# Cross-attention and quantized FFN on one core: row transposes by 32x32 blocks and DRAM instead of DMA transposes, the last projection by rows, and a new order of all steps

## The chip, the core and the metric

The kernel runs on one core of a Trainium2 chip. The metric is device time in microseconds, from several runs of one launch. The engines are named as in the profile: PE multiplies matrices (PEld are its weight loads), DVE and ACT are the vector and the scalar engine, POOL is the general one, and SP issues nearly all DMAs. Each engine works through its own list in order. A difference of about 0.2% is what a measurement of this kernel can tell from none.

## What is computed

Eight batches of 112 rows of 512 go through one layer of cross-attention (16 heads of 128, 375 context rows of 256) and a feed-forward part that works on rounded numbers:

```python
q = rmsnorm(layernorm(x) @ Wq);  k = rmsnorm(ctx @ Wk);  v = ctx @ Wv     # per head
x = x + softmax(q k^T / sqrt(128)) v @ Wo
# feed-forward, n = layernorm(x)
n_q = round(n * 127 / rowmax|n|)                 # per row
h   = gelu((n_q @ W1_q.T) * scales + B1)
h_q = round(h * 127 / rowmax|h|)                 # per row
x   = x + (h_q @ W2_q.T) * scales + B2
```

W1 and W2 are rounded with one maximum for each whole matrix.

## The kernel before, in words

**Tiling.** Batches go in four pairs (NPAIR, BP = 2). For each pair the 16 heads go in four groups of four (NG, HG), so there are 16 groups G, and a unit u is one group of one batch (32 of them). The feed-forward part has 2048 hidden columns in four pieces of 512. A batch has 112 rows in a tile of 128; the 16 spare rows of batches 1 to 7 carry the 112 rows of batch 0.

**Steps of a unit.** Keys (`keys`, L650), copy, squares, sums, root, norm; then keys are turned: DVE transposes 32x32 blocks (L698), four DMAs write them to DRAM (`ks`, L707) and one reads them back in order (`kf`, L714). Queries (L532) take the same way through DRAM (`qt`, `qs`, `qf`). Scores (L758), exponentials on ACT (L780), scaling (L791), blocks on DVE (L797), DRAM (`ps`, `pf`), weighing of the context (`weigh`, L860), values (L887) and projection (`project`, L910), which sums into aT, the transposed output, on DVE (`project_add`, L926). After a pair's last group its aT goes back to rows the same way (`rz`, `rs`, `rf`, `rn`).

**The last pair.** It uses PE transposes in place of the way through DRAM where there is nothing left to hide it: probabilities of the last unit (`pt`, `pk`), and for each batch i of the last pair: values `O{i}`, their copy `U{i}`, projection `P{i}`, its add into aT `A{i}`, transposes of aT `ra` (L965), the residual add `rb` (L1001).

**Feed-forward of a batch b.** `st` takes row means and variances, `fa` to `fd` the root (ln and exp on ACT, the rest on DVE), `fi` (norm_in, L1032) the normed rows and their maximum, `fq` rounds them to bf16. The rounded rows of batches 1 to 5 are transposed by a DMA transpose (`td`, L1073), those of 6 and 7 by PE (`ti`, `tj`). (`b` counts 1 to 7: the rows of batch 0 ride along.) Hidden pieces `h0` to `h3` (L1080), their scale and bias on DVE `i0` to `i3` (L1089), Gelu on ACT (`ge`, or `g0` to `g3` by pieces for the last pair), maximum (`lm`; `mx`, `es`), rounding (`qh0`, `qh1`; `qp`, `qq`), transpose (`te`, the second DMA transpose, L1073; by PE `tp`, `tk` for the last pair), output product (`y0`, `y1`; `Y0` to `Y3`, L1159), `yo` and `yd` the sum and the store.

**What sets the order.** Four strings of words at the end (L1214 to L1364), one for each pair, list all steps in one order, `name.index`; a negative index belongs to the pair before. `play` calls them, and `in_written_order` ties each instruction of PE, DVE, ACT and SP behind the one before it on its engine. So nothing overtakes, and SP's DMAs go out in the list's order. Tiles with the same tag share buffers, so a step can also wait until an earlier user of its tag has been read.

Of the kernel before, what the change touches and what calls it, by code (L numbers as in the profile page):

```python
# [9 lines left out]
F32 = mybir.dt.float32  # L10
# [20 lines left out]
def xattn_ffn_kernel(  # L31
# [16 lines left out]
    nc = tc.nc  # L48
# [853 lines left out]
    def project(G, lo, n, c0):  # L902
        if n == TP:
            after(("u0", G), ("u1", G))
        else:
            after((f"U{lo // S}", G))
        pw = T["pw", G, lo, c0] = mm_tile(f"pw_{G}_{c0}_{lo}")
        for c in range(c0, c0 + NW // n):
            for h in range(HG):
                nc.tensor.matmul(  # L910
                    pw[:, (c - c0) * n : (c - c0 + 1) * n], T["wo", G][:, h, c * P : (c + 1) * P],
                    T["oT", G][:, h, lo : lo + n], start=(h == 0), stop=(h == HG - 1),
                )
# [13 lines left out]

    for n in range(2):
        step(f"o{n}", NG, values, 0, TP, 2 * n)
        step(f"u{n}", NG, value_keep, 0, TP, 2 * n)  # L930
        step(f"p{n}", NG, project, 0, TP, 2 * n)
        step(f"a{n}", NG, project_add, 0, TP, 2 * n)
        step(f"O{n}", NG, values, n * S, S, 0)
        step(f"U{n}", NG, value_keep, n * S, S, 0)
        step(f"P{n}", NG, project, n * S, S, 0)
        step(f"A{n}", NG, project_add, n * S, S, 0)
# [19 lines left out]
    def turn_sum(b):  # L956

        p, i = divmod(b, BP)
        if p == NPAIR - 1:
            after((f"A{i}", NGG - 1))  # L960
        else:
            after(("a0", p * NG + NG - 1), ("a1", p * NG + NG - 1))
# [50 lines left out]
    def stats(b):  # L1013
        after(("rb" if b >= B - BP else "rn", b), ("zf", b))
# [4 lines left out]
    def row_absmax(src, name):  # L1019
        m = small.tile([P, 1], F32, tag="rowmax", name=name)  # L1020
# [8 lines left out]
    def norm_in(b):  # L1029
        after(("fd", b))  # L1030
        xn = T["xn2", b] = ffn.tile([P, C], F32, tag="y", name=f"xn2_{b}")
        nc.vector.tensor_scalar(xn, x2_of(b), T["mv2", b][:, 0:1], T["rstd2", b], ALU.subtract, ALU.mult)  # L1032
        T["m1", b] = row_absmax(xn, f"m1_{b}")
        T["d1", b] = dequant_scale(T["m1", b], absw1, f"d1_{b}")
# [6 lines left out]
    def quantize_in(b):  # L1041
        quantize_rows(home("xq", b, [P, C], BF16), T["xn2", b], quant_scale(T["m1", b], P))
# [27 lines left out]
    def send_rows(b, what):  # L1070

        to = home(what + "T", b, [P, KC if what == "xq" else KF, P], BF16)
        nc.sync.dma_start_transpose(out=to, in_=T[what, b])  # L1073

    def hidden(b, n):
# [3 lines left out]
        for k in range(KC):  # L1079
            nc.tensor.matmul(  # L1080
                ph, T["xqT", b][:, k, :], w1q[:, k, bass.ts(n, NW)], start=(k == 0), stop=(k == KC - 1)
            )

    def hidden_keep(b, n):
        after(("lb", 0))
# [27 lines left out]
    def pieces_scale(b):  # L1113
        after(*[(f"mx{n}", b) for n in range(NF4)])
        m = small.tile([P, 1], F32, tag="rowmax", name=f"m2_{b}")
# [31 lines left out]
    def output(b, k0, n):  # L1147
# [10 lines left out]
        for k in range(k0, k0 + n):  # L1158
            nc.tensor.matmul(  # L1159
                T["py", b], T["hqT", b][:, k, :], w2q[:, k, :], start=(k == 0), stop=(k == KF - 1)  # L1160
# [26 lines left out]
    step("fi", BP, norm_in)  # L1187
    step("fq", BP, quantize_in)
# [3 lines left out]
    step("td", BP, send_rows, "xq")  # L1192
    step("te", BP, send_rows, "hq")
# [13 lines left out]
    for n in range(2):  # L1207
# [7 lines left out]
        cz.0 lk.0 cz.1 lf.0 lf.1 lx.0 l7.0 gl.0 lc.1 kh.0 jl.0 lk.1 lq.0 jl.3 jl.6 kh.1 xs.1 xs.0 xa.1  # L1215
        xc.1 xs.7 ct0.0 kc0.0 xa.0 xb.7 k0.1 kc1.0 xb.1 xd.1 xc.0 xm.1 xa.7 kq0.0 xc.7 k1.1 kr0.0 kq1.0
        kc2.0 xb.0 xd.0 kc0.1 kr1.0 ck0.0 ct0.1 xm.0 kq2.0 xt.1 xd.7 kc1.1 cz.2 xt.0 kr2.0 ck0.1 k2.1
        kb.0 ka.0 xm.7 ke.0 kq0.1 kd.0 xk.0 kn2.0 xt.7 xk.1 gm.0 kn0.0 kv2.0 xk.7 jm.0 kc2.1 xl.0 kv0.0
        kq1.1 lq.1 k0.2 kw0.0 kw2.0 kn1.0 xy.0 xy.1 kr0.1 kv1.0 kr1.1 kq2.1 Q0.0 kr2.1 kb.1 ka.1 jm.3
        kc0.2 ke.1 Q1.0 qt0.0 kw1.0 qs0.0 lx.1 kd.1 jl.1 kn1.1 qv0.0 kn0.1 S0.0 kt0.1 k1.2 kq0.2 kn2.1  # L1220
        S1.0 kt2.1 qw0.0 sa.0 sb.0 kc1.2 kt1.1 k2.2 kq1.2 ks.1 qt1.0 sc.0 qx0.0 sd.0 qv1.0 kr0.2 kc2.2
        k0.3 kr1.2 kq2.2 qs1.0 kr2.2 lc.2 s2.0 lv.0 kb.2 s7.0 ct1.0 qw1.0 lk.2 s1.0 qx1.0 ck1.0 s3.0
        jm.1 kc0.3 s0.0 ka.2 kq0.3 k1.3 ke.2 x0.0 kf.1 k2.3 kc1.3 ly.0 x1.0 e0.0 jl.7 Q0.1 kd.2 e2.0
        kn2.2 e3.0 kn0.2 e1.0 iv.0 xs.3 n0.0 kc2.3 kn1.2 pt0.0 n2.0 k0.4 qt0.1 S0.1 xs.2 qs0.1 n3.0
        kt0.2 kq1.3 pt2.0 pt3.0 pk0.0 kt1.2 n1.0 s1.1 kt2.2 pk2.0 ct1.1 cb0.2 kc0.4 ks.2 s0.1 cb1.2
        pt1.0 kr0.3 s3.1 kr1.3 kq0.4 k1.4 xa.3 pk3.0 jl.2 ck1.1 kr0.4 kq2.3 pk1.0 k2.4 x0.1 xb.3 s2.1
        e0.1 kr2.3 Q1.1 kc1.4 kb.3 ka.3 kc2.4 ke.3 kq1.4 kd.3 kq2.4 kn0.3 xc.3 kf.2 e1.1 x1.1 qf0.1 k0.5
        lq.2 kt0.3 lk.3 e2.1 kn2.3 e3.1 w0.0 xd.3 iv.1 kr1.4 n0.1 n2.1 z0.1 xa.2 qt1.1 w1.0 n1.1 n3.1
        kn1.3 qs1.1 S1.1 z1.1 z3.1 k1.5 z2.1 sb.1 G0.1 xm.3 ps.1 v0.0 kt1.3 s1.2 kr2.4 s2.2 kb.4 ka.4
        kt2.3 ke.4 s0.2 sa.1 xc.2 ks.3 sc.1 s3.2 kc0.5 sd.1 kc1.5 x0.2 k2.5 kq0.5 x1.2 e0.2 lo.0 Q0.2  # L1230
        kq1.5 kr0.5 kc2.5 e3.2 kd.4 kn0.4 kq2.5 e2.2 kn1.4 v1.0 qt0.2 S0.2 k0.6 pf.1 qf1.1 e1.2 cs.2
        Q1.2 kt0.4 qs0.2 kn2.4 kt2.4 iv.2 k1.6 kt1.4 n1.2 kf.3 n0.2 kr1.5 ks.4 n3.2 xb.2 z0.2 S1.2 xd.2
        jm.2 kc0.6 n2.2 lq.3 w0.1 xm.2 G1.1 sa.2 kc1.6 k2.6 qt1.2 qf0.2 z3.2 w1.1 ja.0 z1.2 sb.2 z2.2
        kr2.5 s1.3 v1.1 cz.3 lc.3 v0.1 s2.3 ps.2 ka.5 o0.0 sc.2 js.0 s0.3 kb.5 u0.0 js.1 qs1.2 ke.5 k0.7
        kc2.6 kq1.6 kd.5 s3.3 kn0.5 s7.1 o1.0 x0.3 lk.4 kf.4 kt0.5 e0.3 Q0.3 x1.3 kq0.6 e1.3 kn2.5 u1.0
        G0.2 kr0.6 e2.3 kn1.5 k1.7 kt2.5 pf.2 kt1.5 kr1.6 kc0.7 ks.5 e3.3 k2.7 iv.3 cb0.3 n1.3 qt0.3
        n2.3 Q1.3 lv.1 kc1.7 cb1.3 qs0.3 sd.2 kc2.7 js.2 n0.3 kq2.6 kq0.7 kr2.6 n3.3 qf1.2 s3.4 kr0.7
        ka.6 S0.3 s1.4 z0.3 s0.4 ke.6 z3.3 kq1.7 z1.3 p0.0 kq2.7 z2.3 S1.3 x0.4 ps.3 jr.0 s2.4 sa.3 jr.1
        lk.5 p1.0 kf.5 qt1.3 x1.4 G1.2 qs1.3 w0.2 e0.4 kr2.7 e1.4 kb.6 kd.6 kr1.7 qf0.3 k0.8 pf.3 a0.0
        ka.7 e3.4 lo.1 a1.0 e2.4 sb.3 az.0 k1.8 iv.4 kb.7 n0.4 kn2.6 v0.2 kn0.6 sc.3 kt0.6 z0.4 s3.5  # L1240
        s2.5 xu.2 s1.5 kn1.6 G0.3 s0.5 n3.4 kt2.6 qf1.3 w1.2 n2.4 xv.2 z3.4 kt1.6 z2.4 kc0.8 x0.5 ke.7
        w0.3 ks.6 n1.4 kc1.8 sd.3 kq0.8 jr.2 v1.2 w1.3 e0.5 cs.3 z1.4 G1.3 k2.8 v1.3 v0.3 xu.3 xw.2 jl.4
        x1.5 o0.1 ps.4 kd.7 e2.5 kn0.7 o1.1 kc2.8 kn2.7 kq1.8 kf.6 kn1.7 lq.4 k0.9 js.3 xv.3 xk.2 k1.9
        u0.1 kr0.8 u1.1 xy.2 kr1.8 e3.5 cf.2 kt0.7 s7.2 e1.5 k2.9 kq2.8 iv.5 kt1.7 n2.5 kt2.7 p1.1 n3.5
        cz.4 kr2.8 kc0.9 kq0.9 jm.4 kc1.9 n0.5 pf.4 kc2.9 n1.5 z0.5 ka.8 kq1.9 z3.5 z2.5 kb.8 z1.5 s1.6
        kr0.9 ps.5 s0.6 jr.3 kq2.9 s3.6 p0.1 x0.6 kr2.9 e0.6 kr1.9 ke.8 e1.6 xw.3 jm.6 s2.6 lx.2 Q0.4
        s7.3 ks.7 kd.8 kb.9 a1.1 a0.1 w0.4 qt0.4 S0.4 kn0.8 kn2.8 x1.6 k0.10 pf.5 kn1.8 e2.6 k1.10 xk.3
        ka.9 xy.3 v0.4 xs.4 jl.5 w1.4 qs0.4 xb.4 xa.4 k2.10 kt0.8 lv.2 kt1.8 kf.7 lk.6 kt2.8 kc0.10 ks.8
        xc.4 w0.5 e3.6 xd.4 ke.9 iv.6 kc1.10 kd.9 xs.5 lo.2 w1.5 v0.5 jm.7 kc2.10 v1.4 kq0.10 co0.2 Q1.4
        qf0.4 xa.5 n3.6 n0.6 n2.6 z0.6 v1.5 z3.6 n1.6 jm.5 kq1.10 o1.2 S1.4 s0.7 z1.6 kn0.9 s1.7 kn2.9  # L1250
# [151 lines left out]
```

## Time and profile before

| what | us |
|---|---|
| median of 3 runs (720.21 to 721.2) | 720.77 |
| the profiled run | 720.28 |
| its span, first to last instruction | 718.5 |
| PE busy / DVE busy / ACT busy in it | 702.7 / 537.3 / 433.6 |
| DMA queues, share of 16 engines | 85.1% |
| granted PE clock | 0.999 |

A matmul's end in the profile is modelled, and matmuls overlap: one of 512 columns in f32 is drawn 593 ns long, while the next one starts 429 ns after it. The pace is the distance of the starts, which the chain of work (the profile's fourth part, and its long form in order of time) gives: there each piece counts only up to the start of the next. The idle time of PE is what is left of a stretch after its busy time.

DMA issues that bear on the change (KB of one, median us from issue to landing):

```
rd<-rz SPq DMA_DIRECT2D x24, 64.0 KB, 4.5
rt<-rd SPq DMA_DIRECT2D x6, 256.0 KB, 4.3
xqT<-xq SPq DMA_TRANSPOSE x5, 2.9
hqT<-hq SPq DMA_TRANSPOSE x5, 5.6
```

### The profile page before, as it was taken

The page shows a single profiled execution, that of the slowest core. Times are in us where ns is not written, and L with a number is a line of the kernel's source. Part 1 is how long each engine was busy: PE and PEld are TensorE (multiplying, and loading weights), DVE is VectorE, ACT ScalarE, POOL GpSimd, SP SyncE. Part 2 cuts the span into 40 slices and gives each one's busy share as a digit, 9 for nine tenths or more (in the row PEclk, how much of TensorE's full clock was granted, in tenths as well). Part 3 has the DMA queues.
Part 4 walks back from the last instruction along what each step waited for, and adds up shares of the span by engine and source line. Part 5 has one row for each costly group of instructions (what it writes and reads, how often), then busy time and mean ns, then how long its engine had stood idle before and what let it go on. Part 6 is the DMA issues. An engine that isn't in the chain of part 4 may idle for free.

```text
span 718.5 us, 8555 instructions
## 1 busy us (share of the span) xinstructions
PE 702.7 (98%) x2398; PEld 413.3 (58%) x2410; DVE 537.3 (75%) x1234; ACT 433.6 (60%) x1129; POOL 2.4 (0%) x10
## 2 busy tenths in 40 slices
PE   9999999999999999999999999999999999999976
PEld 4444456655657564745656465564657455667742
DVE  6997888887876677747857787868774898964395
ACT  5677576636475756556466556666755566627325
POOL 0000000000000000000000000000000000000000
PEclk9999999999999999999999999999999999999999
DMA  8799999989988999999898989999999889998201
GB/s 304 266 280 298 294 298 282 301 268 290 282 308 244 293 285 313 269 275 310 227 289 286 295 265 287 287 240 305 292 257 291 237 256 272 259 290 282 34 1 44
DMA packets 131246, 187.85 MB, mean 261 GB/s; under 512 B 34864, under 2 KB 90800, under 8 KB 130560
## 3 DMA queue, kind: packets, MB, share of 16 engines
q1 hardware_dynamic: 131200, 187.32, 85.1%
q8 instruction: 19, 0.31, 0.2%
q14 instruction: 27, 0.22, 0.1%
HBM read 124.55 MB, written 59.45 MB: 256 GB/s over the span
## 4 chain that ended last, share of the span: by engine, by line
PE 85%; DVE 5%; ACT 4%; DMA 3%; SPq 1%; issue 1%; POOL 0%; ACTq 0%; DVEq 0%; POOLq 0%
PE pkk L650 19%; PE pu L860 17%; PE pw L910 13%; PE pq L532 12%; PE sc L758 10%; PE po L887 6%; PE py L1159 2%; PE ph L1080 2%; DMA pT<-pd 1%; PE pkk L660 1%; DMA kT<-kd 1%; ACT probs L780 1%; DMA qr<-q 1%; DMA qss<-s 1%; ACT qsq L547 1%
## 5 line engine op out<-in xcount | busy, mean ns | idle before, releaser
L650 PE MATMUL pkk<-wk,cT 128*128 128x512 f32 x372 | 171.8, 593 | 0.3 <-DVE hid L1089 0.3
L860 PE MATMUL pu<-pT,c 128*128 128x448 f32 (+1 forms) x384 | 152.3, 540 | 1.0 <-DMA pT<-pd 1.0
L860 PEld LDWEIGHTS pu<-pT,c 128*128 128x128 f32 (+1 forms) x384 | 72.5, 190 | 71.3 <-issue 61.7
L780 ACT ACTIVATE probs<-sc,bias,rq 112x375 f32<-112x375 f32 x128 | 84.1, 663 | 47.8 <-DVE bias L773 47.8
L650 PEld LDWEIGHTS pkk<-wk,cT 128*128 128x128 f32 x372 | 70.0, 190 | 72.3 <-issue 60.9
L910 PEld LDWEIGHTS pw<-oT,wo 128*128 128x128 f32 x544 | 98.2, 190 | 9.8 <-issue 6.5
L910 PE MATMUL pw<-oT,wo 128*128 128x224 f32 (+1 forms) x544 | 101.8, 343 | 0.6 <-ACT oT L897 0.6
L532 PE MATMUL pq<-wq,xnT 128*128 128x512 f32 x224 | 100.2, 592 | 0.0
L758 PE MATMUL sc<-kT,qT 128*112 128x384 f32 x256 | 92.4, 486 | 0.3 <-DMA kT<-kd 0.2
L670 ACT COPY kk<-pkk 128x512 f32<-128x512 f32 x96 | 55.2, 580 | 58.6 <-DVE kz L698 25.6
L797 DVE STREAM_TRANSPOSE pz<-probs 128x384 f32<-128x384 f32 x120 | 63.7, 558 | 21.1 <-ACT probs L791 18.2
L791 ACT ACTIVATE probs<-probs,inv 112x375 f32<-112x375 f32 x128 | 72.1, 605 | 8.9 <-DVE inv L788 8.9
L771 DVE TENSOR_REDUCE top<-sc 112x1 f32<-112x375 f32 x128 | 63.8, 535 | 18.0 <-PE sc L758 17.5
L681 DVE TENSOR_REDUCE kss<-ksq 128x4 f32<-128x512 f32 x96 | 63.1, 668 | 14.0 <-ACT ksq L675 14.0
L532 PEld LDWEIGHTS pq<-wq,xnT 128*128 128x128 f32 x224 | 42.4, 190 | 49.6 <-issue 46.5
L758 PEld LDWEIGHTS sc<-kT,qT 128*112 128x112 f32 x256 | 44.7, 177 | 38.9 <-issue 16.7
L675 ACT ACTIVATE ksq<-kk 128x512 f32<-128x512 f32 x96 | 59.5, 628 | 6.4 <-DVE kss L681 6.0
L688 DVE TENSOR_TENSOR kk<-kk,rk 128x512 f32<-128x512 f32 x96 | 62.9, 675 | 0.5
L698 DVE STREAM_TRANSPOSE kz<-kk 128x512 f32<-128x512 f32 x93 | 62.3, 690 | 0.9 <-issue 0.4
L871 ACT COPY wc<-pu 128x448 f32<-128x448 f32 x64 | 33.5, 531 | 36.6 <-PE pu L860 36.6
L887 PEld LDWEIGHTS po<-wc,wv 128*128 128x128 f32 x272 | 49.1, 190 | 8.0 <-issue 4.1
L887 PE MATMUL po<-wc,wv 128*128 128x224 f32 (+1 forms) x272 | 53.1, 344 | 0.0
(122 smaller groups left out, 590.8 us busy)
## 6 DMA issues: line engine op xcount, KB each, us to landing
kd<-kz SPq DMA_DIRECT2D x124, 192.0 KB, 4.0
kT<-kd SPq DMA_DIRECT2D x31, 768.0 KB, 6.4
pT<-pd SPq DMA_DIRECT2D x30, 672.0 KB, 6.1
pd<-pz SPq DMA_DIRECT2D x90, 192.0 KB, 4.4
wq<-in_wq SPq DMA_DIRECT2D x16, 1024.0 KB, 7.7
wo<-in_wo SPq DMA_DIRECT2D x16, 1024.0 KB, 7.8
wv<-in_wv SPq DMA_DIRECT2D x16, 512.0 KB, 5.8
wk<-in_wk SPq DMA_DIRECT2D x15, 512.0 KB, 6.2
```

The source lines that it names most:

```text
L532: nc.tensor.matmul(pq[:, :GW], T["xnT", p][:, k, i * P : (i + 1) * P], T["wq", G][:, k, :], start=(k == 0), stop=(k == KC - 1),)
L650: nc.tensor.matmul(pk[:, :GW], T["cT", batch_of(u)][:, k, j * P : (j + 1) * P], T["wk", u // BP][:, k, :], start=(k == 0), stop=(k == KCC ...
L681: nc.vector.tensor_reduce(T["kss", u][:, j, :], T.pop(("ksq", u, j)).rearrange("p (h d) -> p h d", d=D), AX.X, ALU.add)
L688: nc.vector.tensor_tensor(kv, kv, T["rk", u][:, j, :].unsqueeze(2).to_broadcast([P, HG, D]), ALU.mult)
L758: nc.tensor.matmul(sc[:S, :SKP].rearrange("p (j i r) -> p j i r", j=NJ, r=BK), T["qT", G, i][:, h, :], T["kT", u][:, :, :, h, :].rearrange ...
L771: nc.vector.tensor_reduce(top[:, h : h + 1], T["sc", u, h0 + h][:S, :SK], AX.X, ALU.max, negate=True)
L780: nc.scalar.activation(p_bufs[h][:S, :SK], T["sc", u, h][:S, :SK], AF.Exp, bias=T["bias", u, h0][:, h - h0 : h - h0 + 1], scale=rq_of(u, h ...
L791: nc.scalar.mul(p_bufs[h][:S, :SK], p_bufs[h][:S, :SK], T["inv", u][:, h : h + 1])
L797: nc.vector.transpose(T["pz", u][:, :, :, :, h, :].rearrange("p a f j q -> p j a f q"), p_bufs[h].rearrange("p (j a r) -> p j a r", j=NJ, ...
L860: nc.tensor.matmul(pu[:, : HG * S], T["c", b][: ROWS[j], j, k * P : (k + 1) * P], T["pT", u][: ROWS[j], :, j, :, :].rearrange("p f h q -> ...
L887: nc.tensor.matmul(po[:, (h - h0) * n : (h - h0 + 1) * n], T["wv", G][:, k, h * D : (h + 1) * D], T["wc", G][:, k, h, :, :].rearrange("p b ...
L910: nc.tensor.matmul(pw[:, (c - c0) * n : (c - c0 + 1) * n], T["wo", G][:, h, c * P : (c + 1) * P], T["oT", G][:, h, lo : lo + n], start=(h ...
```

## The change

**Row transposes.** For batches 1 to 5 the two DMA transposes (`td`, `te`) are gone. In their place DVE transposes 32x32 blocks of the rounded rows (`Xz` for xq in one instruction; `Hz0`, `Hz1` for hq in two), four DMAs write them to DRAM (`Xs`, `Hs`), one reads them back (`Xf`, `Hf`). The tiles for the blocks share their tags with the query blocks ("qz") and the key blocks ("kz"). In the fetched tile the index k is innermost, so `hidden` and `output` read their weights with a step of 4 or 16 elements.

```diff
-    def send_rows(b, what):
-        to = home(what + "T", b, [P, KC if what == "xq" else KF, P], BF16)
-        nc.sync.dma_start_transpose(out=to, in_=T[what, b])
+    def row_blocks(b, what, n0, n1):
+        K = KC if what == "xq" else KF
+        if n0 == 0:
+            T["z" + what, b] = work.tile([P, NB, BK, K], BF16, tag="qz" if what == "xq" else "kz", name=f"z{what}_{b}", bufs=1)
+        nc.vector.transpose(
+            T["z" + what, b][:, :, :, n0:n1].rearrange("p a q k -> p k a q"),
+            T[what, b][:, n0 * P : n1 * P].rearrange("p (k a c) -> p k a c", a=NB, c=BK),
+        )
+    def row_send(b, what):
+        K = KC if what == "xq" else KF
+        rd = T["rd" + what, b] = dram.tile([NB, BK, NB, K * BK], BF16, tag="rd" + what, name=f"rd_{what}_{b}")
+        for n in range(NB):
+            nc.sync.dma_start(
+                out=rd[:, :, n, :].rearrange("a c n -> c a n"),
+                in_=T["z" + what, b][n * BK : (n + 1) * BK].rearrange("c a q k -> c a (q k)"),
+            )
+    def row_fetch(b, what):
+        to = home(what + "T", b, [P, P, KC if what == "xq" else KF], BF16)
+        nc.sync.dma_start(
+            out=to.rearrange("p t k -> p (t k)"),
+            in_=T.pop(("rd" + what, b)).rearrange("a c n m -> (a c) (n m)"),
+        )
+    def columns(what, b, k):
+        t = T[what, b]
+        return t[:, k, :] if b >= B - BP else t[:, :, k]
...
-                ph, T["xqT", b][:, k, :], w1q[:, k, bass.ts(n, NW)], start=(k == 0), stop=(k == KC - 1)
+                ph, columns("xqT", b, k), w1q[:, k, bass.ts(n, NW)], start=(k == 0), stop=(k == KC - 1)
...
-                T["py", b], T["hqT", b][:, k, :], w2q[:, k, :], start=(k == 0), stop=(k == KF - 1)
+                T["py", b], columns("hqT", b, k), w2q[:, k, :], start=(k == 0), stop=(k == KF - 1)
```

**Last projection by rows.** `P{i}` and `A{i}` are gone. `R` multiplies with the values as weights, so that rows come out, and `rc` adds them to the residual. `ra` and `rb` now bring in the sum of the groups before the last, and can stand earlier.

```diff
+    def project_rows(i):
+        after((f"U{i}", NGG - 1))
+        pr = T["pr", i] = mm_tile(f"pr_{i}")
+        for h in range(HG):
+            nc.tensor.matmul(
+                pr[:S, :], T["oT", NGG - 1][:, h, i * S : (i + 1) * S], T["wo", NGG - 1][:, h, :],
+                start=(h == 0), stop=(h == HG - 1),
+            )
+    def rows_add(i):
+        x2 = T["x2", NPAIR - 1][:S, i, :]
+        after(("rb", B - BP + i))
+        nc.vector.tensor_tensor(x2, x2, T.pop(("pr", i))[:S, :], ALU.add)
...
-        if p == NPAIR - 1:
-            after((f"A{i}", NGG - 1))
-        else:
-            after(("a0", p * NG + NG - 1), ("a1", p * NG + NG - 1))
+        after(("a0", NGG - 2), ("a1", NGG - 2))
```

**Root beside the rounding.** `fi` subtracts the mean only and no longer waits for the root: the rounded rows do not depend on it. A new step `fe` multiplies the maximum with the root for the scale that `hidden_keep` uses.

```diff
-        after(("fd", b))
+        after(("st", b))
         xn = T["xn2", b] = ffn.tile([P, C], F32, tag="y", name=f"xn2_{b}")
-        nc.vector.tensor_scalar(xn, x2_of(b), T["mv2", b][:, 0:1], T["rstd2", b], ALU.subtract, ALU.mult)
+        nc.vector.tensor_scalar(xn, x2_of(b), T["mv2", b][:, 0:1], None, ALU.subtract)
         T["m1", b] = row_absmax(xn, f"m1_{b}")
-        T["d1", b] = dequant_scale(T["m1", b], absw1, f"d1_{b}")
+    def scale_in(b):
+        after(("fi", b), ("fd", b))
+        m = small.tile([P, 1], F32, tag="rowmax2", name=f"m1r_{b}")
+        nc.vector.tensor_tensor(m, T["m1", b], T["rstd2", b], ALU.mult)
+        T["d1", b] = dequant_scale(m, absw1, f"d1_{b}")
```

**Order.** All four lists are written anew, so every engine's list differs from its start. The end of the last list, before and after:

```diff
-        v0.6 qh0.-1 pt2.7 v1.6 pt1.7 qh1.-1 pk2.7 O0.3 pk1.7 te.-1 w0.7 U0.3 P0.3 v0.7 w1.7 A0.3 ra.0
-        v1.7 O1.3 rb.0 st.0 fb.0 U1.3 fa.0 P1.3 fc.0 fd.0 fi.0 fq.0 A1.3 ti.0 bo.0 ra.1 tj.0 rb.1 h0.0
-        st.1 h1.0 i0.0 fa.1 fc.1 h2.0 i1.0 g0.0 fb.1 h3.0 i2.0 fd.1 g2.0 fi.1 fq.1 i3.0 ti.1 y0.-1 tj.1
+        v1.6 pt2.7 pk0.7 O0.3 pk2.7 n1.7 pt3.7 U0.3 ra.0 pk3.7 Hz0.-1 pt1.7 R.-6 Hz1.-1 rb.0 Hs.-1 pk1.7
+        w0.7 rc.-6 st.0 fi.0 w1.7 v0.7 fq.0 fa.0 fc.0 Hf.-1 bo.0 ti.0 fb.0 v1.7 ra.1 tj.0 fd.0 h0.0 rb.1
+        h1.0 fe.0 i0.0 h2.0 i1.0 g0.0 O1.3 i2.0 g2.0 mx0.0 h3.0 U1.3 mx2.0 g1.0 R.-5 i3.0 mx1.0 g3.0
+        mx3.0 es.0 qp0.0 qp2.0 qq0.0 y0.-1 rc.-5 st.1 fi.1 fa.1 y1.-1 fq.1 fc.1 qq2.0 qp1.0 ti.1 tp0.0
+        tj.1 tk0.0 yo.-1 h0.1 qq1.0 fb.1 yd.-1 fd.1 h1.1 fe.1 i0.1 h2.1 i1.1 g0.1 h3.1 qp3.0 i2.1 tp1.0
```

(`R.-6` and `R.-5`, `rc.-6` and `rc.-5` are R.0, R.1, rc.0 and rc.1 of the text.) In the new list the root of batch 7 (`fa.1`, `fc.1`) stands on ACT between Gelus of batch 6 and of batch 7. At the start, a second piece of W1 and the context of batch 2 are loaded ahead of the first query weights.

## The prediction

> **What bounds the kernel now.** I read the engine totals first, then the table of busy time by stretches of 20 us (the six columns after the stretch: its length, PE, PE weight loads, DVE, ACT, POOL; then granted clock, DMA share and GB/s).
>
> ```profile
> PE 702.7 (98%) x2398; PEld 413.3 (58%) x2410; DVE 537.3 (75%) x1234; ACT 433.6 (60%) x1129; POOL 2.4 (0%) x10
> ...
> 560.00:580.00 20.00, 19.01 (x49) 8.91 (x49) 17.18 (x41) 13.80 (x39) 0.00 (x0) 1.00 0.86 257
> ...
> 660.00:680.00 20.00, 20.00 (x110) 15.12 (x109) 8.26 (x13) 8.72 (x18) 0.00 (x0) 1.00 0.47 113
> 680.00:700.00 20.00, 15.46 (x97) 9.86 (x99) 17.94 (x47) 5.01 (x10) 0.00 (x0) 1.00 0.00 1
> 700.00:718.50 18.50, 11.63 (x72) 5.45 (x71) 11.04 (x24) 10.06 (x18) 0.00 (x0) 0.96 0.14 43
> ```
>
> PE is the bound, and its idle time has three places: 2.3 us in the first 60 us, 2.1 us in the 620 us after them (the stretch shown, at 560, is the worst, 0.99 us), and 11.4 us after 680. But a busy PE may be a slow one, so I next took its pace from the chain that ended last, where a row gives time and number of matmuls.
>
> ```profile
> 383.58 6.05 PE pw L910 x32
> 389.63 3.43 PE pkk L650 x8
> ...
> 408.74 4.52 PE pu L860 x12
> ...
> 458.87 2.58 PE sc L758 x8
> ...
> 536.94 1.73 PE py L1159 x8
> ...
> 673.42 3.56 PE pw L910 x32
> ```
>
> That is 0.189 us for a record 224 wide, 0.429 for f32 512 wide, 0.376 for 448, 0.322 for 384, 0.216 for bf16 512, and 0.111 for the 112-wide ones of the last projection (an f32 matmul leaves two records). Times the counts: pkk 384 x 0.429 = 164.7; pq 224 x 0.429 = 96.1; pu 384 x 0.376 = 144.4; sc 256 x 0.322 = 82.4; 720 records 224 wide 136.1; 96 records 112 wide 10.8; 224 bf16 ones 48.4; warm-up 3.8; transposes about 9.9. Sum 696.6 us of 718.5. So PE runs at its pace almost everywhere; what can be won is the other 21.9 us: 5.6 at the ends (1.2 before the first matmul, 4.4 after the last), 6.8 in stalls up to 663, and 9.6 in stalls of the tail.
>
> Third, the tail in order of time:
>
> ```profile
> 682.31 3.83 PE L910 MATMUL pw<-oT,wo 128*128 128x112 f32 x32 [0.62 <-ACT oT L897]
> ...
> 686.85 0.65 PE L965 MATMUL pa<-ident,aT 128*112 128x128 f32 x4 [0.34 <-DVE aT L926]
> ...
> 694.65 0.40 PE L1052 MATMUL pxq<-ident_h,xq 128*128 128x128 bf16 x4 [3.24 <-DVE xq L1039]
> ```
>
> The last batch goes projection, add on DVE, four transposes, add, LayerNorm, quantization before PE gets it back; the longest stall (3.24 us) is that.
>
> **Last projection by rows.** Removed: 64 records of 0.111 = 7.1 us of PE. Added: 16 records 512 wide, 6.9 us. PE work is the same (696.3). What goes is a link: the add into aT (0.62 us on DVE) and the four transposes (0.44 to 0.65 us) with their handovers; the transposes and the first residual add now come before this projection, with the sums of the groups before. LayerNorm's root (two ACT steps, four DVE steps, 683.30 minus 681.35 = 1.95 us here) leaves the way to the quantized rows; it is needed only for the first scale and add of hidden_keep. In exchange fe adds two small DVE steps (0.16 + 0.21), hidden under the first hidden matmuls.
>
> **The tail of the new order, by the rows of this trace.** I start at 663.3, where the last group's weighing of batch 6 begins in both orders, with 41.0 us of matmul work left in the new one (41.2 in the old). Weighing 4.5, two turns 0.6, ACT copy and values: 670.5. Transposes and turns, then R.0: 671.5 to 674.95. On DVE ahead of its add: the two halves of batch 5's blocks (1.2 to 1.35 each, below), the residual add and a copy, so rc.0 ends at 676.1. Stats 0.69 + 0.18, subtract 0.55, maximum 0.69, scale 0.15 twice, quantize 0.49 + 0.43 and 0.04 between: 679.7; PE has had 4.5 us of weighing until then. Transpose, bias add 0.68 and a copy 0.42 ahead: hidden of batch 6 at 681.1, with O1.3 (1.8) inside to 686.4; R.1 686.4 to 689.85; the last stage's output of batch 5 (16 x 0.216) to 693.3. DVE, busy with the maxima, reaches rc.1 at 690.5, so xq of batch 7 is ready at 694.9: a stall of 1.6 us where 3.24 stood. Hidden of batch 7 ends at 699.6 (701.7 before), its last add at 701.3 (703.5 before). ACT now has three table loads more there (1.28 us each by the profile's row), because the root of batch 7 falls between two Gelus; they put the first add of batch 7 0.8 us later, which is in these times. From that add to the last matmul the old order took 10.6 us; by the new one's list I get 10.0. The last matmul ends at 711.3 instead of 714.1: **minus 3 us**.
>
> **No DMA transposes.** The rows (duration ns min/median/max; below, issue to landing):
>
> ```profile
> L1159 PEld LDWEIGHTS <-hqT x112: 95/98/98, 362.5 to 713.7; 128*128 128x128 bf16 x112
> L1073 SPq DMA_TRANSPOSE hqT<-hq x5: 1323/3762/5465, 349.8 to 669.4; - x5
> DMA to landing us min/median/max: 4.7/5.6/7.5
> ```
>
> ```profile
> kd<-kz SPq DMA_DIRECT2D x124, 192.0 KB, 4.0
> kT<-kd SPq DMA_DIRECT2D x31, 768.0 KB, 6.4
> ```
>
> Removed are ten issues: five of 1.2 us (xq, landing 2.9) and five of 3.8 us, some 25 us of SP's queue. SP is in order: pT, kT and weight loads stand behind them. Added: fifty plain issues at about 0.44 us, 22 us, in shorter pieces, each last one waiting for the first four to land. Latency rises: 4 us to DRAM and 4 to 6 back, where 2.9 and 5.6 stood. Bytes (3.2 MB out and in, of 188) change little. Weighed against the Trainium skill: "DMA: Bandwidth & Descriptors", Rules for kernel authors, says to use the hardware's DMA transpose and not a plain DMA with a rearranged pattern, 19 times slower. By it, xq would land after 19 x 2.9 = 55 us, and the hidden matmuls, some 4 to 10 us of PE work behind the fetch in the new list, would stall by over 40 us for each of five batches. The rows speak otherwise, because DVE has turned the 32x32 blocks and the DMA only moves runs: the same route carries the keys in 4.0 + 6.4 us. I take the rows. The fetch then has 3.6, 3.8, 9.2, 6.2 and 4.3 us of PE work before hidden, for at least 3 us of landing; 0 to 1.5 us each in the first two, I take 0.5 in all. Output has 9 us or more everywhere.
>
> **DVE's blocks.** Five of 128x512 and ten of 128x1024, bf16, written with a step of 8 and 32 bytes. Nearest rows: f32 blocks, 384 wide 558 ns and 512 wide 690 ns, so 0.69 and 1.2 each: 15.5 us on an engine with 181 us idle. No row writes at such a step; low end half of it (2-byte data), high end double. I take the row. The tiles share buffers with the query and key blocks: the next key transposes stand 3.4 us (batch 1) to 10 us of PE work behind the send, which lands in 4; there DVE waits up to 1 or 2 us with the key path queued behind it, hidden by the 12 us (median) that the new order leaves between a key fetch and its first score.
>
> **Strided weights.** PE now loads xqT and hqT with a step of 4 and 16 elements. Trace: 98 ns packed, under a matmul pace of 216. "Advanced Engine Details and Errata", SBUF Cachelines, says that a line is 16 bytes and two hits on it are needed for full rate; xq has two, hq one. No row here shows such a load. Doubled it is 196, still hidden: 0. At four times, 80 loads of hq would cost 176 ns each, 14 us. By the packed row 0; I take 0 and keep 14 as the far end.
>
> **Ordered anew.** I added up, in both lists, the PE work between a fetch's place and its first reader. Key fetch to score: shortest 3.9 us before, 5.7 after, median 7.8 and 12.2; probability fetch to weighing: 3.0 and 3.9, median 6.5 and 8.8; weight loads are earlier too. In the trace the stalls on such transfers are 1.16 us at 574 (3.4 us of cover) and 0.3 at 638 (3.9). With the new cover I expect most of the 3.2 us of stalls between 230 and 660 to go, and some DVE waits in their place: minus 1.5 (plus 3 to minus 3). At the start, 1.4 MB more stand ahead of the first wq: at the 304 GB/s of the first slice it lands some 4.5 us after the 17.0 of before, where PE wants it near 21.3; the 0.6 us wait on the first keys goes: 0 (minus 0.5 to plus 2).
>
> **Sum.** 718.5 - 3.0 - 1.5 + 0.5 = 714.5 of span. The profiled run took 720.28 for 718.5; the median shown is 720.77, so 0.3 to 0.5 above it. 714.5 + 1.8 + 0.2 = **716.5 us**.
>
> **Rivals.** (1) The order wins nothing in the middle: DVE's new waits for landed sends take the place of the DMA stalls, and the start loses 1: 719 to 720. For it: the list leaves less cover between send and fetch (median 7.6 us, 11.7 before). Against it: that delays SP alone. 25%. (2) Slower: strided block writes at twice the row. Price: 2.4 us in the tail, where rc.0 and the copy of the last probabilities are queued behind the two hq halves and PE waits for both; and at five places in the middle 1 to 1.5 us of PE's wait behind a DVE that is 80 to 90% busy there (18.4 of 20 us at 580): 716.5 + 2.4 + 5 = 724. It decides from about 1.9 times the row. 18%. (3) Strided weights at four times: 731, 5%; part of it is that with them the change gives PE more to do than it takes.
>
> **Chances.** Forecast 52%: from 713 to 719. A measurement tells about 0.2% (1.4 us) from no change: 719.3 to 722.2. Faster 0.52 + half of rival 1 = 0.64; same 0.13; slower 0.23. Range 712.5 to 725: it leaves out rival 3 and the ends.
>
> **What would show it.** Right: the stall before the batch-7 transpose near 1.6 us, last matmul near 711 on the old scale; middle stretches at 19.9 or more; new blocks near 0.69 and 1.2 us; weight loads under 216 ns. Wrong: blocks over 2 us, py or ph over 216 ns apart, or PE stalls released by DVE in the middle.

## The result

| kernel | median us | runs | profiled run, span | PE clock |
|---|---|---|---|---|
| before | 720.99 | 4 | 720.28, 718.5 | 0.999 |
| changed | 747.98 | 4 | 745.01, 743.2 | 0.991 |

The changed kernel takes 1.037 times as long (95% interval 1.034 to 1.040): 27 us slower, where 716.5 was forecast. (Of the runs below, one of the four of e2 took 1515 us; its ratio is that of the other three, with a median of 714.58.) The engine totals and stretches of the profile after, with the columns as before:

```profile
PE 709.1 (95%) x2362; PEld 415.1 (56%) x2362; DVE 585.6 (79%) x1256; ACT 437.7 (59%) x1132; POOL 2.4 (0%) x10
...
360.00:380.00 20.00, 16.07 (x40) 7.65 (x39) 17.24 (x30) 11.23 (x38) 0.00 (x0) 0.91 0.84 224
480.00:500.00 20.00, 16.71 (x58) 9.50 (x58) 19.65 (x34) 11.19 (x33) 0.00 (x0) 1.00 0.79 241
...
540.00:560.00 20.00, 17.46 (x52) 10.08 (x51) 16.73 (x41) 10.38 (x26) 0.00 (x0) 0.91 0.82 246
...
640.00:660.00 20.00, 15.32 (x75) 12.39 (x73) 19.21 (x42) 7.17 (x20) 0.00 (x0) 1.00 0.77 225
...
700.00:720.00 20.00, 16.81 (x65) 9.04 (x66) 16.65 (x36) 6.52 (x12) 0.00 (x0) 0.83 0.18 52
```

PE, idle for 15.8 us before (718.5 - 702.7), is idle for 34.1 now, and it idles in the middle, where the worst stretch had cost 0.99 us. In those stretches DVE is busy for 17 to 20 of 20 us. PE is also busy for 6.4 us longer, and in some stretches its granted clock is below 1. DVE's total rose by 48 us, not by the 15.5 reckoned. The rows of the new blocks and of the weight loads (duration ns min/median/max; below each row of blocks, us from issue to landing of its sends) say why:

```profile
L1092 DVE STREAM_TRANSPOSE zhq<-hq x10: 4475/4539/4714, 349.5 to 697.5; 128x1024 bf16<-128x1024 bf16 x10
...
DMA to landing us min/median/max: 2.0/2.3/2.9
...
L1092 DVE STREAM_TRANSPOSE zxq<-xq x5: 1310/1321/1331, 293.9 to 631.0; 128x512 bf16<-128x512 bf16 x5
...
DMA to landing us min/median/max: 2.3/4.0/5.2
...
L1201 PEld LDWEIGHTS <-hqT x112: 95/143/154, 389.1 to 738.5; 128*128 128x128 bf16 x112
...
L1122 PEld LDWEIGHTS <-xqT x112: 95/113/138, 307.5 to 727.7; 128*128 128x128 bf16 x112
```

A half of hq takes 4.54 us, 3.8 times the 1.2 of the row that was used; a block of xq takes 1.32, 1.9 times its 0.69. Ten and five of them make 52 us. The weight loads grew to 143 and 113 ns and stay under the pace. PE's waits name who released it (us in total, times, longest):

```profile
PE pu L860 <- DVE pT L834: 6.0, 1, 6.0
PE ph L1122 <- DMA xqT<-rd_xq: 4.1, 2, 3.0
PE pq L532 <- DVE aT L923: 3.9, 1, 3.9
PE sc L758 <- DMA kT<-kd: 2.5, 2, 2.1
PE sc L758 <- ACT probs L780: 2.4, 1, 2.4
PE pu L860 <- DVE aT L923: 2.2, 1, 2.2
```

None of these names the blocks. The longest one, followed in DVE's timeline (start, duration, what):

```profile
692.94 0.51 DVE L834 COPY pT<-pp 128x336 f32<-128x336 f32 x1 [3.71 <-PE pp L827]
693.36 8.77 DVE L1092 STREAM_TRANSPOSE zhq<-hq 128x1024 bf16<-128x1024 bf16 x2
701.78 0.86 DVE L1010 TENSOR_TENSOR x<-x,pa 112x512 f32<-112x512 f32 x1
702.57 0.48 DVE L834 COPY pT<-pp 128x336 f32<-128x336 f32 x1
```

The copy of the last probabilities, 0.48 us long, was late because two blocks of 8.77 us stood in front of it. DVE had stood idle for 3.71 us shortly before them. The wait of 3.9 us is of the same kind: an add into aT stands behind a block on DVE, and PE's query matmuls wait for it (two lines of DVE, one of PE):

```profile
359.84 4.50 DVE L1092 STREAM_TRANSPOSE zhq<-hq 128x1024 bf16<-128x1024 bf16 x1
...
363.98 0.81 DVE L923 TENSOR_TENSOR aT<-aT,pw 128x448 f32<-128x448 f32 x1
...
364.84 1.50 PE L532 MATMUL pq<-wq,xnT 128*128 128x512 f32 x2 [3.93 <-DVE aT L923]
```

So is the wait for kT at 658 us: the chain leads from it to the key blocks (647.9) and on to zhq, on which DVE worked from 633.4 to 642.3.

### The profile page after: what moved, and what is told of

Same layout as the page of the kernel before. It is cut to its first block, busy times and chain, and to the rows that moved or that the text cites. A ratio compares the mean times of both kernels' runs of the same rounds, so it can differ in the third digit from the quotient of the medians.

```text
span 743.2 us, 8585 instructions
## 1 busy us (share of the span) xinstructions
PE 709.1 (95%) x2362; PEld 415.1 (56%) x2362; DVE 585.6 (79%) x1256; ACT 437.7 (59%) x1132; POOL 2.4 (0%) x10
## 4 chain that ended last, share of the span: by engine, by line
PE 58%; DVE 19%; DMA 12%; SPq 5%; ACT 4%; issue 3%; DVEq 0%; ACTq 0%
PE pu L860 14%; PE pkk L650 13%; PE pq L532 8%; PE sc L758 8%; PE pw L907 7%; DVE zhq L1092 5%; PE po L887 4%; DMA pd<-pz 2%; PE ph L1122 2%; DMA kT<-kd 2%; DVE pz L797 2%; DVE kss L681 1%; DMA kd<-kz 1%; PE py L1201 1%; DMA xqT<-rd_xq 1%
## 5 line engine op out<-in xcount | busy, mean ns | idle before, releaser
L860 PE MATMUL pu<-pT,c 128*128 128x448 f32 (+1 forms) x384 | 154.7, 548 | 8.8 <-DVE pT L834 6.0
L532 PE MATMUL pq<-wq,xnT 128*128 128x512 f32 x224 | 102.4, 601 | 3.9 <-DVE aT L923 3.9
L758 PE MATMUL sc<-kT,qT 128*112 128x384 f32 x256 | 95.2, 490 | 6.0 <-DMA kT<-kd 2.5
L907 PEld LDWEIGHTS pw<-oT,wo 128*128 128x128 f32 x480 | 90.7, 190 | 10.8 <-issue 5.3
L907 PE MATMUL pw<-oT,wo 128*128 128x224 f32 x480 | 95.1, 353 | 0.8 <-DVE hid L1131 0.8
```

What stands on the lines that cost most here:

```text
L532: nc.tensor.matmul(pq[:, :GW], T["xnT", p][:, k, i * P : (i + 1) * P], T["wq", G][:, k, :], start=(k == 0), stop=(k == KC - 1),)
L758: nc.tensor.matmul(sc[:S, :SKP].rearrange("p (j i r) -> p j i r", j=NJ, r=BK), T["qT", G, i][:, h, :], T["kT", u][:, :, :, h, :].rearrange ...
L860: nc.tensor.matmul(pu[:, : HG * S], T["c", b][: ROWS[j], j, k * P : (k + 1) * P], T["pT", u][: ROWS[j], :, j, :, :].rearrange("p f h q -> ...
L907: nc.tensor.matmul(pw[:, (c - c0) * n : (c - c0 + 1) * n], T["wo", G][:, h, c * P : (c + 1) * P], T["oT", G][:, h, lo : lo + n], start=(h ...
```

## Experiments

Theory (a): DVE's writes with a distance between elements are the loss. Rivals: (b) bf16 blocks are slow as such, (c) other work slows them, (d) the way through DRAM is too long, (e) the new order loses. The time of the kernel before was 721.9 to 722.6 in these runs, each set on one chip; sets are compared by their ratio to it. In e1, e6, e7, e12 and e13 the elements of a row arrive in another order, with the same work; the others of the table compute everything.

| run | median us | ratio to before (95%) |
|---|---|---|
| e1, no distance | 715.63 | 0.992 (0.989 to 0.995) |
| e2, DMA transposes, new order | 715.01 | 0.989 (0.986 to 0.992) |
| e3, runs of 64 bytes in DRAM | 759.29 | 1.051 (1.049 to 1.054) |
| e4, pairs as 32-bit elements | 716.54 | 0.991 (0.988 to 0.994) |
| e5, before + rows alone | 722.11 | 1.000 (0.998 to 1.002) |
| e6, distance in batch 5's hq only | 725.37 | 1.004 (1.002 to 1.006) |
| e7, distance in xq only | 718.23 | 0.995 (0.994 to 0.997) |
| e12, distance in hq of batches 1 to 4 | 738.26 | 1.023 (1.021 to 1.026) |
| e13, as e6, one half earlier | 720.67 | 0.998 (0.996 to 1.000) |
| e8, e4 with the root waited for | 720.90 | 0.997 (0.996 to 0.999) |
| e9, e4 with columns | 724.15 | 1.002 (1.000 to 1.004) |
| e10, e4 with a move at the start | 718.26 | 0.995 (0.993 to 0.997) |
| e11, e2 with that move | 716.42 | 0.993 (0.990 to 0.995) |

**The blocks by themselves.** A small kernel, in outline:

```python
for step in (1, 4, 8, 16):               # h: bf16, 512 and 1024 wide; f: f32
    z = const.tile([P, NB, BK, step], dt)          # step 1: [P, NB, K, BK]
    nc.vector.transpose(z[..., :K].rearrange("p a q k -> p k a q"), rows)
```

> A small kernel that only copies x to the output and then, with nothing beside it, turns 32x32 blocks on DVE (128x512 and 128x1024, bf16 and f32) with several distances between written elements, copies with such distances, and loads weights with distances of 1 to 32 elements. All of the layer is left out; only durations of single instructions count. Theory (a), the distance between written elements is what costs: bf16 128x1024 takes about 4.5 us at 16 elements but about 1.0 to 1.2 at 1, 128x512 about 1.3 us at 4 and 0.5 to 0.7 at 1; f32 shows the same rise at the same distance in bytes. Rival (b), bf16 blocks are slow by themselves: over 1.2 and over 4 us at every distance. Rival (c), the rest of the kernel slows them (other engines on the same memory): here all under 1.2 us. Weight loads: 98 ns packed, near 113 at 4 and 143 at 16, with the matmuls 216 ns apart in all of them.

The groups of DVE (the last number but one is the mean in ns), three instructions each but two in the sixth line, in the order bf16 512 at 1, 4, 8, 16 elements; bf16 1024 at 16; f32 512 at 1, 4, 8:

```profile
L106 DVE STREAM_TRANSPOSE h_step<-hrc 128x512 bf16<-128x512 bf16 x3 | 2.1, 711 | 0.1
L106 DVE STREAM_TRANSPOSE h_step<-hrc 128x512 bf16<-128x512 bf16 x3 | 3.9, 1312 | 0.1
L106 DVE STREAM_TRANSPOSE h_step<-hrc 128x512 bf16<-128x512 bf16 x3 | 7.5, 2492 | 0.1
L106 DVE STREAM_TRANSPOSE h_step<-hrc 128x512 bf16<-128x512 bf16 x3 | 7.1, 2381 | 0.1
L106 DVE STREAM_TRANSPOSE h_step<-hrc 128x1024 bf16<-128x1024 bf16 x3 | 13.5, 4512 | 0.1
L106 DVE STREAM_TRANSPOSE f_step<-src 128x512 f32<-128x512 f32 x2 | 1.4, 712 | 0.1
L106 DVE STREAM_TRANSPOSE f_step<-src 128x512 f32<-128x512 f32 x3 | 3.2, 1064 | 0.1
L106 DVE STREAM_TRANSPOSE f_step<-src 128x512 f32<-128x512 f32 x3 | 3.3, 1087 | 0.1
```

Packed bf16 costs what f32 costs, 711 ns for 512. With distance it rises to 2.6 ns an element at 8 bytes and 4.4 to 4.9 at 16 and 32; f32 at 16 and 32 bytes costs 2.1. I had expected the same rise for f32 at the same distance; it rose 1.5 times, and bf16 3.3 times and more. (b) and (c) fall: packed blocks are fast, and the scattered ones take as long here, beside little else, as in the changed kernel. TensorE ran most of this kernel at half clock (0.697 on average), so its weight loads say nothing here.

**No distance, all else the same (e1); the order and DMA transposes (e2).** The main lines of each edit:

```diff
 (e1)
-            T["z" + what, b] = work.tile([P, NB, BK, K], BF16, ...)
+            T["z" + what, b] = work.tile([P, NB, K, BK], BF16, ...)
-            T["z" + what, b][:, :, :, n0:n1].rearrange("p a q k -> p k a q"),
+            T["z" + what, b][:, :, n0:n1, :].rearrange("p a k q -> p k a q"),
 ...
 (e2)
+    def row_send(b, what):
+        to = home(what + "T", b, [P, KC if what == "xq" else KF, P], BF16)
+        nc.sync.dma_start_transpose(out=to, in_=T[what, b])
 ...
```

> As the changed kernel, but DVE writes each turned run of 32 without a distance; sends, fetches and strided weight loads stay byte for byte as many and as long. What is left out: the elements of a row arrive in another order, so the feed-forward multiplies wrong pairs; its work is the same. Theory (a), DVE's block writes are the loss: ten blocks fall from 4.5 to about 1.1 us, five from 1.3 to 0.6, some 37 us of DVE less, PE stalls in the middle and before the last values mostly gone, 717 to 726 us. Rival (d), the way through DRAM is too long: 738 to 745, the stalls on fetches at 437 and 643 us stay. Rival (e), the new order itself loses: over 740.

> As the changed kernel with its order, its last projection by rows and its root, but the rounded rows go by DMA transposes as before, issued at the place of the send; no block work on DVE. Theory (a) and rival (d): 714 to 722 us, with PE stalls only where the ten transposes hold SP's queue. Rival (e), the order itself loses: 735 or more. Against the run with unscattered writes it prices the way through DRAM with cheap blocks: by (a) within 4 us of each other, by (d) over 12 apart.

Both came out at (a)'s end, e1 a little below what was expected: 715.6 and 715.0. In e1 the blocks take what the prediction took (those of xq 0.71 us):

```profile
L1092 DVE STREAM_TRANSPOSE zhq<-hq x10: 1201/1232/1247, 348.9 to 673.2; 128x1024 bf16<-128x1024 bf16 x10
```

So one edit, with the same sends, fetches and strided weights, takes the changed kernel from 1.037 to 0.992. (d) and (e) fall. What is left of the change is rows, root and order that together win 6 to 8 us by the ratios, and a way through DRAM for which no gain over DMA transposes is shown: by the ratios e2 is 2 us ahead of e1, and e11 1.6 us ahead of e10, with overlapping intervals.

**Two versions that compute everything (e3, e4).** Neither scatters 16-bit elements.

```diff
 (e3: no distance on DVE, short runs in the sends)
+        rd = T["rd" + what, b] = dram.tile([BK, NB, K, NB, BK], BF16, ...)
+                out=rd[:, :, :, n, :].rearrange("c a k q -> c (a k) q"),
 ...
 (e4: pairs; W1's and W2's rows are loaded in pairs to fit)
+            T["z" + what, b] = work.tile([P, NB, BK, K // 2], F32, ...)
+            T[what, b].bitcast(F32)[:, n0 * P : n1 * P].rearrange("p (k a c) -> p k a c", a=NB, c=BK),
 ...
```

> As the changed kernel, but DVE writes each turned run of 32 without a distance and the sends to DRAM put runs of 64 bytes in their places (in place of 256 and 1024 bytes), so that the fetched tile has packed weights; everything is computed. Theory (a): DVE as in the run before it, and if short runs do not slow the sends, 716 to 726 us, a version near or better than both kernels. If the sends are slowed by short runs (2048 of them for each quarter of hq), landing goes from 2.3 us to 5 or more, and the stalls move to the fetches: 725 to 745. Rival (e): over 740.

> As the changed kernel, everything computed, but two neighbouring rounded numbers are moved as one 32-bit element: half as many elements for DVE, and W1's and W2's rows are laid out in pairs to fit. From the measurement of single instructions, 32-bit elements at 32 bytes cost 2.1 ns in place of 4.4 for 16-bit ones, so a half of hq takes 1.1 us (4.5 in the changed kernel), and a block of xq 0.4 to 0.6. Theory (a), the cost of the distant 16-bit writes is the whole loss: 714 to 718 us, beside 715.6 with unscattered writes. If distance in bytes alone set the cost of a block (not the number of elements), the halves would stay over 2 us and the time over 722. Rival (e), the order: over 740.

e3 lost more than was expected of it, 759. Landing of hq's sends rose to 4.7 us and each issue held SP for 1.03 us (medians; 3.98 the longest), where 2.9 and 0.43 stood in e1; PE waited 11 and 9 us on fetched xq and 7 and 5 on fetched hq (loads and matmuls), and 9.6 on fetched probabilities, and DVE 12.4 us for the sends to free the key buffer. So with DVE's blocks as cheap as in e1 (1.23 us), the short runs in the sends bring a loss of their own, in SP and the transfers. e4 keeps the long runs and halves the number of elements:

```profile
L1096 DVE STREAM_TRANSPOSE zhq<-hq x10: 1066/1094/1111, 347.9 to 672.6; 128x512 f32<-128x512 f32 x10
```

716.5 us (0.988 to 0.994 of before), correct pairing included, is a version of the changed kernel that beats both kernels; e2 does too, and the two cannot be told apart.

**Where the loss sits (e6, e7, e12) and why the tail costs so much (e13).** All are e1 with the distance brought back for some blocks; e13 is e6 with one word moved:

```diff
-        ... v0.6 qh1.-1 n3.7 pt0.7 v1.6 ... ra.0 pk3.7 Hz0.-1 pt1.7 R.-6 Hz1.-1 rb.0
+        ... v0.6 qh1.-1 Hz0.-1 n3.7 pt0.7 v1.6 ... ra.0 pk3.7 pt1.7 R.-6 Hz1.-1 rb.0
```

> The run with unscattered writes, but the two halves of hq of batch 5, the last ones, are written with the distance of the changed kernel. What is left out: in the other batches the elements of a row arrive in another order, with the same work. Theory (a): two halves of 4.5 us in place of 1.2 stand ahead of the copies of the last probabilities, and PE waits for all of the 6.6 us: 721 to 722.5 us against 715.6. By the price that the prediction put on the tail (2.4 us): 718. If PE has other cover there: 716.

> The run with unscattered writes, but the five blocks of xq are written with the distance of the changed kernel (1.3 us in place of 0.7). What is left out: the elements of a row of hq arrive in another order, with the same work. Theory (a) with the price set by DVE's time: 0.6 us five times, of which part is covered: 715.6 to 718 us. If the stalls on the fetched xq (5.1 us in the changed kernel: 1.2 at 437, 3.2 at 643, 0.2 at 306) come from its own blocks: 719 to 721; if they come from DVE being late by the blocks of hq, they stay away here.

> The run with unscattered writes, but the hq blocks of batches 1 to 4 are written with the distance of the changed kernel (eight halves of 4.5 us), batch 5 and xq not. What is left out: in the other blocks the elements of a row arrive in another order, with the same work. Theory: the losses add up. Unscattered 715.6, tail alone 725.4 (9.8), xq alone 718.2 (2.6), the changed kernel 748.0: that leaves 20 us for the middle, 734 to 737 us. If the parts strengthen each other (a late DVE makes all later parts worse): below 731.

> The run with the distance only in the two halves of batch 5, but the first half stands right behind the rounding of hq in DVE's list, where DVE stood idle for 4.0 us, in place of behind the first copy of the last probabilities. DVE's work is the same. What is left out: in the other blocks the elements of a row arrive in another order. If the place in the list makes the loss: PE's stall of 6.2 us falls to about 2.3, too short for the clock to be halved after it, 718.5 to 720.5 us in place of 725.4. If DVE's time itself makes it: over 723.

By ratios, over e1's 0.992: batch 5 adds 0.012, xq 0.003, the middle 0.031; together 1.038, and the changed kernel has 1.037. So the losses add up, 23 us of them in the middle. The profiled runs split them. Against e1 (13.6 us idle, 700.4 busy), PE is idle for 6.8 us more in e6, 12.5 in e12 and 1.2 in e7, together 20.5, and 20.5 more in the changed kernel. And with the same matmuls it is busy for 4.6, 7.0, 1.3 and 8.7 us more. Most of that is a slower PE: the mean clocks of e6, e12 and the changed kernel are 0.994, 0.992 and 0.991, where e1 has 1.000, which by estimate (what is missing from 1.000, times the span) is 4.4, 5.9 and 6.7 us. With xq alone scattered PE's longest wait for a fetched xq (3.0 us in the changed kernel) stays away, and in e12, with packed xq, it is there again (3.0 us): it came from the hq blocks on DVE, not from xq's way.

The tail's two halves cost 8.7 us by the ratios (9.7 by the medians), more than the 6.6 us of DVE that they add and than was expected. The table by stretches of e6 shows the rest (the column after POOL is the granted clock):

```profile
675.00:680.00 5.00, 3.40 (x8) 1.06 (x6) 5.00 (x2) 0.00 (x0) 0.00 (x0) 1.00 0.00 0
680.00:685.00 5.00, 0.55 (x1) 0.50 (x2) 4.99 (x4) 0.00 (x0) 0.00 (x0) 0.80 0.12 26
685.00:690.00 5.00, 5.00 (x8) 2.19 (x7) 4.00 (x10) 0.67 (x2) 0.00 (x0) 0.51 0.64 179
```

After its 6.0 us of waiting PE is busy, but at half clock: 8 matmuls in 5 us. In e13 the same DVE work is done, one half of it in the idle 4 us; PE's wait is 2.5 us and half of the loss is gone (720.7). I had expected no halved clock after so short a stall; e13's table shows 0.66 for the 5 us after it, so that part of the expectation failed:

```profile
675.00:680.00 5.00, 2.52 (x7) 0.74 (x5) 5.00 (x4) 0.00 (x0) 0.00 (x0) 1.00 0.02 6
680.00:685.00 5.00, 5.00 (x9) 2.52 (x10) 4.51 (x11) 0.93 (x3) 0.00 (x0) 0.66 0.64 170
```

It is not so in every run: the four of e13's twelve with a clock of 1.000 took 717.3 to 720.2 us, the five with 0.996 or 0.997 took 719.4 to 723.1.

**What won the tail (e5, e8, e9), and the start (e10, e11).**

```diff
 (e5, in the kernel before)
-        te.-1 w0.7 U0.3 P0.3 v0.7 w1.7 A0.3 ra.0 v1.7 O1.3 rb.0 st.0 fb.0 U1.3 fa.0 P1.3 ...
+        te.-1 ra.0 rb.0 ra.1 rb.1 w0.7 U0.3 R.-6 v0.7 w1.7 rc.-6 v1.7 O1.3 st.0 fb.0 U1.3 fa.0 R.-5 ...
 (e8, in e4; likewise for batch 7)
+        rc.-6 st.0 fa.0 fc.0 fb.0 fd.0 fi.0 w1.7 v0.7 fq.0 ...
 (e9, in e4; likewise for batch 7)
+        U0.3 pk3.7 Hz0.-1 pt1.7 P0.3 Hz1.-1 Hs.-1 pk1.7 w0.7 A0.3 ra.0 rb.0 st.0 ...
 (e10, e11: at the start)
-        qs0.0 ke.1 S0.0 kd.1 ... kn0.1 qw0.0 S1.0 ... sa.0 qx0.0
+        qs0.0 ke.1 qw0.0 qx0.0 S0.0 kd.1 ... kn0.1 S1.0 ... sa.0
```

> The kernel before with its order and DMA transposes; only the last projection goes by rows, with the transposes of the earlier sum and the first residual add ahead of the last values. The root stays where it was. The prediction gave the tail of the new order 3 us; with unscattered writes it came out some 4.5 us shorter (last matmul at 709.4 for 713.9, with a start that was later). If the rows do it: 717 to 718.5 us beside 721 of before. If it is the root beside the rounding and the order of the tail that do it: within 1 us of before.

> The run with pairs, but for the last two batches the rounded rows wait for the root again, as in the kernel before (the root's steps stand ahead of norm_in, which multiplies with it). Last projection by rows as it is. The tail from 640 us on holds 4.7 us of PE stalls in the run with pairs and 10.0 in the kernel before; rows alone in the old order changed nothing. If the root is what won the tail: its 1.95 us come back for both batches where PE waits for xq, the stall before the batch-7 transpose goes from 1.14 to about 3.1 us, 718 to 719.5 us beside 716.5. If the order of the tail did it: within 0.5 us of the run with pairs.

> The run with pairs, but the last projection goes by columns again: 64 matmuls of 112, an add into the transposed sum, and the transposes and the residual add after it, in the new order of the tail. If the rows are worth a link of the chain in the new order: 1 to 2 us slower than the run with pairs (716.5), with a longer stall before the batch-7 transpose (1.14 there) and one before the hidden product of batch 6. If they are worth nothing, as alone in the old order: within 0.5 us.

> The run with pairs with one move at the start: the transposes and the copy of the first query tile stand ahead of the sums of its squares, on PE and ACT. In the run with pairs PE waits 1.24 us for that copy at 30.8 us; the new order holds 4.0 us of PE stalls in the first 40 us, the old one 1.3. If this wait is the end of its chain: 1.2 us faster than the run with pairs, some 715.3. If PE then waits for the keys or the query copy instead: the same.

> The run with DMA transposes in the new order with the same move at the start: 1.2 us below the 715.0 of that run if the wait is real, else the same. Beside the pairs with the same move it says what the way through DRAM is worth against DMA transposes once DVE's blocks are cheap: by the prediction, the same within 1.5 us.

The transposes of batch 7's xq and PE's wait before them, in e4, e5, e8 and e9 in turn:

```profile
694.05 0.40 PE L1071 MATMUL pxq<-ident_h,xq 128*128 128x128 bf16 x4 [0.97 <-DVE xq L1057]
```
```profile
696.55 0.40 PE L1064 MATMUL pxq<-ident_h,xq 128*128 128x128 bf16 x4 [3.23 <-DVE xq L1051]
```
```profile
696.81 0.61 PE L1077 MATMUL pxq<-ident_h,xq 128*128 128x128 bf16 x4 [3.56 <-DVE xq L1063]
```
```profile
702.50 0.61 PE L1073 MATMUL pxq<-ident_h,xq 128*128 128x128 bf16 x4 [2.61 <-DVE xq L1059]
```

With rows and with the root aside the wait is 0.97 us; take either away and it is 3.56 or 2.61, and the transposes after it run at half clock (0.61 us for 0.40). Rows alone in the old order leave 3.23 and 1.000: they win only with the rest. In e8 a table load of ACT (1.28 us) now stands on the chain as well. Both losses, some 4 and 8 us by the ratios, are larger than expected. Much of that is the clock: against e4, PE is idle for only 1.4 us more in e8 and 4.4 in e9, but busy for 3.8 and 6.6 us more, and e4's five runs have clocks of 0.999 and 1.000, those of e8 0.994 to 0.998 and of e9 0.992 to 0.998. In e9 PE also waits 2.08 us for xq of batch 6, and the clock is at 0.50 from 704 to 708. e5 has one place for its new steps; another order around the rows alone was not tried. The move at the start failed: in e10 PE then waits 0.73 us for the same copy at 30.7 and 0.47 for a key copy at 33.1, and e10 and e11 are not faster than e4 and e2.

## Why the prediction was wrong, step by step

- **What bounds the kernel**: right. In e1 PE is busy for 700.4 of 714.0 us.
- **DVE's blocks: the step that failed.** "No row writes at such a step; low end half of it (2-byte data), high end double. I take the row." The row was right for packed writes (1.23 and 0.71 us in e1), but the step makes it 4.54 and 1.32, and for hq the far end of "double" was short too. And the working let DVE's 181 idle us stand for cover: in the middle it put the blocks' cost to PE at nothing, but there they stand in front of short steps that PE waits for. Both show as the signs of being wrong that it named, blocks over 2 us and PE stalls behind DVE in the middle. Of the reason for the cost it had a part in hand, and applied it to PE's loads only: SBUF Cachelines of the page "Advanced Engine Details and Errata" in the Trainium skill. By the 16 bytes of that page, hq's writes go to a line of their own and xq's two to a line. The page says that at least two hits on a line are needed; on DVE the two hits of xq still cost 1.9 times (1.32 us), so two are not enough there. Nor does the line alone explain the cost: f32 with one write to a line took 1064 ns for what bf16 with one took 2492 (m1). Why 16-bit writes cost so much stays open.
- **Rival 2** had the mechanism, the sign and both places. Its price was for twice the row: 2.4 us in the tail and 5 in the middle. At 3.8 times they measured about 9 (e6) and 23 (e12). In proportion to DVE's time (3.3 us more each half, not 1.2) they would be 6.6 and 14, and PE's idle time did rise by 6.8 and 12.5 us; what is beyond that is mostly PE's lower clock (4.6 and 7.0 us more of busy time in the profiled runs), which the working lacked.
- **Way through DRAM**: right. Latencies of 2.3 to 5.0 us (xq's fetch 3.7, not the 55 that the prediction weighed), and neither worth nor loss is shown (e1 against e2). The stalls on fetched xq in the changed kernel were late sends, not long ones. e3 shows the limit of "DMA only moves runs": runs of 64 bytes made it 44 us worse than e1.
- **Strided weights** (rival 3 at four times): right at 0, with 143 and 113 ns; e1 has them and e2 does not, and they are 2 us apart by the ratios, with overlapping intervals.
- **Tail, minus 3**: the mechanism held where DVE was cheap. PE's idle time from 640 us on falls from 11.4 to 7.0 in e1, 1.4 us more than forecast, and the wait before batch 7's transposes is 0.98 where 1.6 was given.
- **Order, minus 1.5, and start, 0**: mis-sized. From 40 to 640 us PE's idle time goes from 2.8 to 2.2 in e1, so 0.6 was won; in e4 it is 2.8, and nothing was. The first 40 us lose 2.7 (1.6 to 4.3; rival 1 had 1 of it), not by a wait for wq (pq starts at 22.9 in e1 and 22.3 before, both times right after transposes that waited for DVE), but mostly by waits for copies and norms on ACT and DVE (0.95, 0.61 and 1.08 us) and one of 0.50 for context rows.
- **Sum**: 714.5 of span by the working, 714.0 in e1, and that is luck. The tail's gain (4.4), the middle's (0.6) and the start's loss (2.7) leave 2.3 us less of PE idle time. The other 2.2 us is PE's busy time, 700.4 for 702.7, which the working left as it was. The clock (0.999 before, 1.000 in e1) is some 0.7 of it by estimate; what the rest is, no run here shows.

## What to carry to other kernels

A block that is laid out anew is costed with its write pattern, not by its shape alone: where no row shows the distance and the element size, it is an unknown (here the far end was 3.8 times), and a small kernel settles it. An added instruction on an in-order engine costs what is queued behind it at that place; look for the idle time beside it (moving one half by a few words took back half of the tail's loss). A PE stall of a few us can be followed by matmuls at half clock, so it can cost more than its length.

## What was not expected of the hardware

Scattered writes of 16-bit elements cost twice those of 32-bit ones at the same distance (4.4 to 4.9 against 2.1 ns an element), so a half of hq moved as pairs in 32-bit elements takes 1.09 us (e4), where 16-bit elements take 4.54 scattered and 1.23 packed. A DVE copy of 128x1024 bf16 with the same distance of 32 bytes took 2.29 us for 0.49 packed, and 4.60 on ACT (m1).

The clock: in the changed kernel PE's wait of 3.9 us at 361 was followed by 8 query matmuls in 5.40 us, for 3.45 elsewhere, in the chain in order of time:

```profile
339.72 3.45 PE pq L532 x8
...
364.84 5.40 PE pq L532 x8
```

The clock was halved after waits of 6.0, 3.9 and 2.4 us in the changed kernel (the last at 543), 3.56 (e8), 2.61 (e9) and 2.5 us (e13). It was not after 3.24 in the kernel before (1.00 from 690 to 700), nor after 3.0 in the changed kernel (at 644; 1.00 from 640 to 660). So the length of a wait alone does not decide. Nor does the kernel: of the 49 runs of the kernel before beside e8 to e11, 15 have a mean clock of 0.995 and a median time of 724.9 us, 10 have 0.999 and 721.5. The Trainium skill, "TensorE: Matmul & The Clock Gate", Part 1, gives an idle window of about 3.4 us that runs freely of the kernel; a free-running window fits a threshold that differs from case to case, but 2.4 us is shorter than the page's window. No run here shows the window itself.
